# A four-layer graph network on one core: the last two batches' layer-1 projections split and moved, part stores issued by GpSimd, one pace for the list steps

## The chip, the cores and the metric

The kernel runs on one core of a Trainium2 chip. The metric is the device time in microseconds (us) of one execution; the median of three runs stands for a kernel. One further execution is taken with the hardware profiler, and all durations below come from that one.

## The reference, cut to what matters

`x` has 16 batches of 1024 nodes with 256 features in float32; `adj` is 1024 x 1024 with about 17 weighted entries in a row. Four layers follow each other.

```python
# layer 0: a score for every pair (u, v), used only where adj is not zero
hidden = relu(pre_u[:, :, None, :] + pre_v[:, None, :, :] + b1)
S = sigmoid(einsum('buvk,ko->buvo', hidden, W2)[..., 0] + b2[0])
a_t = einsum('buv,bud->bvd', S * A_a, h_t)
z_t = beta1 * h_t + beta2 * (a_t @ Wa + ba) + beta3 * (m_t @ Wm + bm)
# layer 1
msg = einsum('bid,ed->bie', einsum('ij,bjd->bid', A, z), W) + b
z = z + relu(msg)
# layers 2 and 3: softmax over all j of leaky_relu(f1[i] + f1[j]) + adj, then
vals = einsum('bij,bjo->bio', coefs, feats); out = vals + bias2 + data
```

## The kernel before, in words

The 16 batches are worked in four groups of four (`GB = 4`, L20). For each group the scores of layer 0 are computed only for the entries that `adj` has, by a side stream of "list steps" on VectorE, ScalarE and GpSimd (`score_steps`, L717), and scattered into a dense array in DRAM. Beside it TensorE does the matrix work. The `Side` class (L882) mixes the two streams as the program is written: the main stream yields an estimate of its own microseconds, and so many list steps are put in as a pace says.

For a group the main stream does this:

- `with_edges` (L1120) sums the scored edges of layer 0. The node columns are taken in four quarters of 256 (`QN`); in each quarter eight accumulators, that is all eight PSUM banks, take eight blocks of source nodes. Each block is loaded by SyncE (`load_gd`, L904), turned by ScalarE or VectorE (`gc`, L1131 and L1133), and multiplied. After a quarter VectorE adds the eight banks to `z` (L1156).
- `layer_one` (L1206) is layer 1 for two batches: `projected` (L1161) multiplies `z` by the weight of layer 1 into node-major tiles `y`, and `neighbours` (L1189) multiplies `y` by `adj`, whose blocks come from DRAM through SyncE into a pool of three buffers (L1195). `onto` (L1182) applies the relu on ScalarE and adds to `z` on VectorE (L1187).
- `front` (L1004) and `sums` (L1085) are the two attention layers. `sums` has VectorE make weighted tiles `m` (L1099), three ahead (`AHEAD`, L34), which TensorE multiplies. After half of the nodes the ends of `second` or `third` follow.

In the last group (g = 3) there are no scores left to compute, so the side stream is another one. `far_ahead` (L1405) first projects batches 2 and 3 of the group (`projected` with a `keep` that also stores `y` to DRAM, L1408), then does their `neighbours` for the last 256 columns, and then layers 1 to 3 of batches 0 and 1 (`pair_layers`, L1340). Beside these, `by_lists` (L1211) forms the neighbour sums of the first 768 nodes (`FAR = 6` tiles of 128) of batches 2 and 3 by lists: GpSimd gathers rows of the stored `y` by index (L708), VectorE multiplies each by its weight and adds (L1246, L1248). It has 144 steps: 24 for six tiles of extra rows (nodes with more than 16 neighbours), whose sums go to a DRAM array `part_d` by SyncE (L1252), 96 for the six tiles themselves, and 24 that gather from `part_d` and add (L1244). A step's gather is issued four steps ahead (`LEAD`), into a pool of six buffers. The pace is written at L1416: 0.68 steps for each estimated microsecond of the main stream while that stands below 82, then 0.61. When the lists are done, `from_lists` (L1255) turns the sums back through TensorE (L1265), and layers 2 and 3 of batches 2 and 3 end the program.

The `paced` helper (L123) makes an instruction wait for the matrix product that was written some products earlier, six unless another number is given, so that a side stream doesn't run ahead of TensorE. Each engine runs its instructions in order; a DMA waits on the engine that issues it, and what is queued behind it on that engine waits too. A `product` (L130) is in float32 and stands in the trace as two records.

The projection loop as it is, whose place changes:

```python
for jt in range(0, NT, 2):
    for i in range(2):
        ps = bank()
        ... four products of 128x256 into ps ...
        nc.scalar.activation(y[i][:, jt : jt + 2, :], ..., AF.Copy)
        if keep:
            keep(i, slice(jt, jt + 2), y[i][:, jt : jt + 2, :])
```

Of the kernel before, what the change touches and what calls it, by code (L numbers as in the profile page):

```python
# [11 lines left out]
F32 = mybir.dt.float32  # L12
# [5 lines left out]
P = 128  # L18
# [52 lines left out]
def gnn_stack_kernel(  # L71
# [616 lines left out]
    with tc.If(listed > 0) as arm:  # L688
        with ExitStack() as stack:
# [427 lines left out]
            def exponential(jt):  # L1117
                paced(nc.scalar.activation(ea[:, jt, :], ea[:, jt, :], AF.Exp), 16)

            def with_edges(g, hw, z):  # L1120

                doing[0] = "edges"
                for v in range(N // QN):
                    cols = slice(v * QN, (v + 1) * QN)
                    acc = [[bank() for _ in range(DH)] for _ in range(GB)]
                    for ut in range(NT):
                        gd = first_gd.pop(0) if first_gd else load_gd(g, v, ut, back=BACK)
                        gc = gc_pool.tile([P, GB, QN], F32, tag="gc", name="gc")
                        by_batch = gd.rearrange("p n i -> p i n")
                        if ut % 2:  # L1130
                            paced(nc.vector.tensor_copy(gc, by_batch), 16)  # L1131
                        else:
                            paced(nc.scalar.activation(gc, by_batch, AF.Copy), 16)  # L1133
                        for i in range(GB):
                            for eh in range(DH):
                                product(
                                    acc[i][eh][:, :QN], hw[i][:, ut, eh * P : (eh + 1) * P], gc[:, i, :],
                                    start=ut == 0, stop=ut == NT - 1,
                                )
                        if z_loads and ut % 2 == 0:  # L1140
                            load, i = z_loads.pop(0)
                            paced(load(i), 12)
                        if (to_load or to_exp) and ut % 2 and v:
                            if v > 1 and to_exp:
                                exponential(to_exp.pop(0))
                            if to_load:
                                jt = to_load.pop(0)
                                paced(nc.sync.dma_start(ea[:, jt, :], adjT_d[jt]), 16)
                                to_exp.append(jt)
                        yield 3.4 if g or v else 1  # L1150
                    if v == N // QN - 1:
                        while to_exp:
                            exponential(to_exp.pop(0))
                    for i in range(GB):
                        for eh in range(DH):
                            nc.vector.scalar_tensor_tensor(  # L1156
                                z[i][:, eh, cols], acc[i][eh][:, :QN], zbias[:, eh : eh + 1], z[i][:, eh, cols],
                                ALU.add, ALU.add,
                            )

            def projected(z, keep=None):  # L1161

                doing[0] = "one"
                y = [node_major("y") for _ in range(2)]
                for jt in range(0, NT, 2):
                    for i in range(2):
                        ps = bank()
                        for k in range(2):
                            for dh in range(DH):
                                product(  # L1170
                                    ps[:, k * D : (k + 1) * D], z[i][:, dh, (jt + k) * P : (jt + k + 1) * P],
                                    l1wT[:, dh, :], start=dh == 0, stop=dh == DH - 1,
                                )
                        nc.scalar.activation(
                            y[i][:, jt : jt + 2, :], ps.rearrange("p (t d) -> p t d", t=2), AF.Copy
                        )
                        if keep:
                            keep(i, slice(jt, jt + 2), y[i][:, jt : jt + 2, :])
                        yield 1.7
                return y  # L1180

            def onto(z, cols, sums):  # L1182
# [6 lines left out]
            def neighbours(y, z, cols):  # L1189
                doing[0] = "one"  # L1190
                n = cols.stop - cols.start
                acc = [[bank() for _ in range(DH)] for _ in range(2)]
                for jt in range(NT):
                    a = three.tile([P, HN], F32, tag="a", name="adjT_in")[:, :n]
                    nc.sync.dma_start(a, adjT_d[jt][:, cols])  # L1195
                    for i in range(2):
                        for eh in range(DH):
                            product(
                                acc[i][eh][:, :n], y[i][:, jt, eh * P : (eh + 1) * P], a,
                                start=jt == 0, stop=jt == NT - 1,  # L1200
                            )
# [9 lines left out]
            def by_lists(msg):  # L1211

                spares = [gd_pool.tile([P, QN, GB], F32, tag="gd", name="msg") for _ in range(4)]
                halves = [
                    t.rearrange("p n i -> p (n i)")[:, k * 2 * D : (k + 1) * 2 * D] for t in spares for k in range(2)
                ]
                msg.extend(halves[:FAR])
                part = halves[FAR:]
                nc.gpsimd.memset(part[0], 0.0)
                nc.sync.dma_start(part_d[XT * P :, :], part[0])  # L1220

                nc.vector.tensor_scalar(to_u, to_u, float(XT * P), None, ALU.min)
                todo = [(NT + i, k) for i in range(XT) for k in range(QUAD)]
                todo += [(t, k) for t in range(FAR) for k in range(FIRST)]
                todo += [(t, FIRST + q) for t in range(FAR) for q in range(NG)]
                got = {}

                def fetch_row(t, k):
                    z = got[t, k] = slot_pool.tile([P, GB * D], F32, tag="z", name="z")[:, : 2 * D]
                    if t < NT and k >= FIRST:  # L1230
                        at = (k - FIRST) * NT + t
                        gather(z, part_d, to_u[:, at : at + 1])
                    else:
                        gather(z, y_d, lists(t)[1][:, k : k + 1])

                for step in todo[:LEAD]:
                    fetch_row(*step)
                for n, (t, k) in enumerate(todo):
                    if n + LEAD < len(todo):
                        fetch_row(*todo[n + LEAD])  # L1240
                    z = got.pop((t, k))
                    to = msg[t] if t < NT else part[t % len(part)]
                    if t < NT and k >= FIRST:
                        paced(nc.vector.tensor_tensor(to, to, z, ALU.add))  # L1244
                    elif k == 0:
                        paced(nc.vector.tensor_scalar(to, z, lists(t)[3][:, k : k + 1], None, ALU.mult))  # L1246
                    else:
                        paced(nc.vector.scalar_tensor_tensor(  # L1248
                            to, z, lists(t)[3][:, k : k + 1], to, ALU.mult, ALU.add
                        ))  # L1250
                    if t >= NT and k == QUAD - 1:
                        nc.sync.dma_start(part_d[(t - NT) * P : (t - NT + 1) * P, :], to)  # L1252
                    yield

            def from_lists(z, msg):  # L1255
# [146 lines left out]
                if g in finished:  # L1402
                    first_gd.extend(load_gd(g, 0, ut) for ut in range(4))

            def far_ahead(z, main):  # L1405

                both = y_d.rearrange("(t p) (i d) -> p t i d", p=P, i=2)
                y = yield from projected(z, lambda i, ts, y: nc.sync.dma_start(both[:, ts, i, :], y))  # L1408
                gone, far = 0.0, Side(by_lists(msg))
                rest = neighbours(y, z, slice(FAR * P, N))  # L1410

                def slots():
                    nonlocal gone
                    for us in itertools.chain(rest, main):
                        gone += us
                        yield us * (0.68 if gone < 82 else 0.61)  # L1416

                far.along(slots(), dict.fromkeys(PACE, 1))
                for _ in far.steps:
# [147 lines left out]
```

## Time and profile before

| | us |
|---|---|
| median of 3 runs | 3126.28 |
| lowest and highest run | 3121.62, 3131.03 |
| the profiled execution, its time | 3123.77 |
| the profiled execution, its span | 3122.0 |
| TensorE busy in the span | 3071.5 (98%) |
| VectorE busy | 2422.3 (78%) |
| GpSimd busy | 1894.7 (61%) |
| ScalarE busy | 1821.7 (58%) |

A record "PE" is a matrix product, "PEld" the loading of its weights, which runs beside it. "SPq" and "POOLq" are DMAs that SyncE and GpSimd issue. In brackets behind an instruction stands how long its engine had been idle and what ended that. In a table of stretches, "PEclk" is the clock that was granted to TensorE and "DMA share" the mean busy share of the 16 DMA engines. The last group's stretches, in us from the start of the span: edge sums of all four batches 2594 to 2706, projections of batches 2 and 3 to 2720, their last 256 columns to 2735, projections of batches 0 and 1 to 2755, their neighbours to 2811, their layers 2 and 3 to 2962, and layers 2 and 3 of batches 2 and 3 to the end.

### The profile page before, as it was taken

To read this page: it belongs to the slowest core of one execution; us is meant where nothing else is said; L and a number is where in the kernel's file an instruction comes from. 1 tells how busy PE (TensorE), PEld (TensorE's weight loads), DVE (VectorE), ACT (ScalarE), POOL (GpSimd) and SP (SyncE) were. 2 spreads that over 40 slices of the span, in tenths; PEclk is the share of its full clock that TensorE was granted. 3 is DMA by queue.
4 is the path that set the end of the run, shared out by engine and by line. 5 is a ranking of instruction groups with operands and counts; after the bars stand their busy time and mean duration, and the time that the engine had idled before them with its cause. 6 is when DMAs were issued, how large, how long until landed. Compare 5 with 4: busy or idle time off the path is not lost. (4 is left out here: it accounts for less than half of the span.)

```text
span 3122.0 us, 39040 instructions
## 1 busy us (share of the span) xinstructions
PE 3071.5 (98%) x11954; PEld 2181.0 (70%) x11954; DVE 2422.3 (78%) x3247; ACT 1821.7 (58%) x6456; POOL 1894.7 (61%) x1483
## 2 busy tenths in 40 slices
PE   8999999999999999999999999999999999999999
PEld 5544545545547756888875688887568888858888
DVE  7887777778776878999887899988789983257844
ACT  3345555566655766777667677766667762214242
POOL 1156778777665777667677776676777751076600
PEclk9999999999999999999999999999999999999999
DMA  9998888888889777558977655897765554475500
GB/s 322 330 339 302 278 296 266 272 248 254 263 268 347 233 224 209 155 163 279 304 234 214 201 160 166 271 301 236 215 196 157 165 205 158 137 254 158 162 1 28
DMA packets 288420, 699.96 MB, mean 224 GB/s; under 512 B 46141, under 2 KB 141178, under 8 KB 281034
## 3 DMA queue, kind: packets, MB, share of 16 engines
q0 software_dynamic: 128224, 387.80, 42.0%
q1 hardware_dynamic: 132538, 258.46, 23.5%
q10 hardware_dynamic: 27440, 51.13, 4.4%
q8 instruction: 96, 1.57, 0.2%
q14 instruction: 122, 1.00, 0.1%
HBM read 565.83 MB, written 131.41 MB: 223 GB/s over the span
## 5 line engine op out<-in xcount | busy, mean ns | idle before, releaser
L831 ACT ACTIVATE z<-z 128x256 f32<-128x256 f32 x2432 | 979.7, 406 | 585.6 <-DVE z L827 523.0
L825 DVE TENSOR_TENSOR z<-z,u 128x1024 f32<-128x1024 f32 x608 | 738.3, 1219 | 299.1 <-PE bank L131 174.4
L131 PE MATMUL bank<-feats,m 128*128 128x257 f32 x4096 | 908.7, 380 | 1.1 <-ACT feats L1016 0.7
L708 POOL DMA_INDIRECT z<-v_d,slot_v x512 | 665.4, 1300 | 367.1 <-ACT z L831 196.8
L131 PEld LDWEIGHTS bank<-feats,m 128*128 128x128 f32 x4096 | 769.5, 190 | 111.1 <-ACT feats L1016 1.5
L713 POOL DMA_INDIRECT dense_d<-gt,slot_at x512 | 682.5, 1333 | 196.4 <-issue 139.3
L827 DVE SCALAR_TENSOR_TENSOR z<-z,w2r 128x1024 f32<-128x1024 f32 x608 | 737.3, 1219 | 9.3
L131 PE MATMUL bank<-gc,hw 128*128 128x256 f32 x2048 | 451.1, 382 | 14.9 <-ACT gc L1133 10.2
L831 ACT ACTIVATION_READ_ACCUMULATOR z<-z 128x1 f32 x2432 | 461.6, 190 | 0.0
L131 PE MATMUL bank<-adj_sb,h 128*128 128x512 f32 x1024 | 443.0, 592 | 4.4 <-ACT st L333 2.1
L131 PEld LDWEIGHTS bank<-gc,hw 128*128 128x128 f32 x2048 | 388.8, 191 | 76.8 <-ACT gc L1133 13.3
L1099 DVE SCALAR_TENSOR_TENSOR m<-rho,tau,adj_sb 128x512 f32<-128x512 f32 x512 | 375.7, 742 | 66.0 <-PE bank L131 61.7
L131 PE MATMUL bank<-adjT_in,y 128*128 128x512 f32 (+1 forms) x960 | 402.0, 579 | 5.3 <-DMA adjT_in<-adjT_d 3.6
L131 PEld LDWEIGHTS bank<-adj_sb,h 128*128 128x128 f32 x1024 | 194.1, 190 | 244.8 <-issue 239.0
L131 PEld LDWEIGHTS bank<-adjT_in,y 128*128 128x128 f32 x960 | 181.5, 190 | 219.4 <-issue 206.4
L131 PE MATMUL bank<-w,hT 128*128 128x512 f32 (+1 forms) x1024 | 334.0, 486 | 0.0
L131 PEld LDWEIGHTS bank<-w,hT 128*128 128x128 f32 x1024 | 194.5, 190 | 140.9 <-issue 121.9
L1133 ACT ACTIVATE gc<-gd 128x1024 f32<-128x1024 f32 x64 | 133.2, 2082 | 169.9 <-PE bank L131 104.2
L131 PE MATMUL bank<-g_wT,z 128*128 128x257 f32 x1024 | 230.1, 380 | 0.0
L131 PEld LDWEIGHTS bank<-g_wT,z 128*128 128x128 f32 x1024 | 192.2, 190 | 30.0 <-issue 2.9
L708 POOL DMA_INDIRECT z<-v_d,x_node x96 | 125.0, 1303 | 116.8 <-ACT z L831 61.0
L1131 DVE COPY gc<-gd 128x1024 f32<-128x1024 f32 x64 | 71.8, 1122 | 105.8 <-PE bank L131 79.3
(169 smaller groups left out, 2439.1 us busy)
## 6 DMA issues: line engine op xcount, KB each, us to landing
gd<-dense_d SPq DMA_DIRECT2D x128, 512.0 KB
dense_d<-zero ACTq DMA_DIRECT2D x64, 512.0 KB
adjT_in<-adjT_d SPq DMA_DIRECT2D x112, 256.0 KB
h<-in_x_dram SPq DMA_DIRECT2D x19, 1024.0 KB
u_d<-st SPq DMA_DIRECT2D x64, 256.0 KB
v_d<-st SPq DMA_DIRECT2D x64, 256.0 KB
hw_d<-st SPq DMA_DIRECT2D x64, 256.0 KB
u<-u_d POOLq DMA_DIRECT2D x32, 512.0 KB
```

Source lines behind the costliest of these rows:

```text
L131: recent.append(nc.tensor.matmul(*args, **kw))
L708: return nc.gpsimd.indirect_dma_start(out=dst, out_offset=None, in_=src[:], in_offset=bass.IndirectOffsetOnAxis(ap=at, axis=0), **how,)
L713: return nc.gpsimd.indirect_dma_start(out=dst[:], out_offset=bass.IndirectOffsetOnAxis(ap=at, axis=0), in_=src, in_offset=None,)
L825: paced(nc.vector.tensor_tensor(z, z, u, ALU.add))
L827: nc.vector.scalar_tensor_tensor(zk, zk, 0.0, w2r[:, None, :].to_broadcast([P, GB, D]), ALU.max, ALU.mult)
L831: nc.scalar.activation(zk[:, c, :], zk[:, c, :], AF.Copy, accum_out=s[:, k, c : c + 1])
L1099: nc.vector.scalar_tensor_tensor(m, r[:, cols], ta[:, kt : kt + 1], ea[:, kt, cols], ALU.max, ALU.mult)
L1131: paced(nc.vector.tensor_copy(gc, by_batch), 16)
L1133: paced(nc.scalar.activation(gc, by_batch, AF.Copy), 16)
```

## The change

It does four things, the first three in the last group alone.

1. The projection becomes a class with a method `pair(q)` that does two node tiles for both batches. `with_edges` takes a function `between`. In the last group `pair(0)` follows the second quarter of the edge sums and `pair(1)` the third; `pair(2)` and `pair(3)` stay where all four were. Their stores of `y` to DRAM go with them. A `y` tile now holds both batches for half of the node tiles rather than one batch for all; this holds in every group.
2. The sums of the extra rows are stored by GpSimd, three list steps after they are done, instead of by SyncE at once. Their two buffers lie in a tile of the `gc` pool instead of in the fourth tile of the `gd` pool.
3. The gathers from `part_d` follow each tile's own 16 steps, instead of standing at the end for all six tiles.
4. The pace of the list steps is 0.64 for each estimated microsecond throughout.

```diff
-            def with_edges(g, hw, z):
+            def with_edges(g, hw, z, between=None):
...
+                    if between and 0 < v < N // QN - 1:
+                        yield from between(v - 1)
...
-            def projected(z, keep=None):
-
-                doing[0] = "one"
-                y = [node_major("y") for _ in range(2)]
-                for jt in range(0, NT, 2):
+            class Projection:
...
+                def __call__(self, i, jt):
+                    return self.halves[jt // HT][:, i, jt % HT, :]
+
+                def pair(self, q):
+
+                    if q % 2 == 0:
+                        t = ttile("y")[:, : 2 * HT * D]
+                        self.halves.append(t.rearrange("p (i t d) -> p i t d", i=2, t=HT))
                     for i in range(2):
                         ps = bank()
                         for k in range(2):
+                            jt = 2 * q + k
                             for dh in range(DH):
                                 product(
-                                    ps[:, k * D : (k + 1) * D], z[i][:, dh, (jt + k) * P : (jt + k + 1) * P],
+                                    ps[:, k * D : (k + 1) * D], self.z[i][:, dh, jt * P : (jt + 1) * P],
                                     l1wT[:, dh, :], start=dh == 0, stop=dh == DH - 1,
                                 )
...
+                        nc.scalar.activation(y, ps.rearrange("p (t d) -> p t d", t=2), AF.Copy)
+                        if self.keep:
+                            self.keep(i, slice(2 * q, 2 * q + 2), y)
                         yield 1.7
...
-                part = halves[FAR:]
+                free = gc_pool.tile([P, GB, QN], F32, tag="gc", name="part").rearrange("p i n -> p (i n)")
+                part = [free[:, : 2 * D], free[:, 2 * D :]]
...
-                todo += [(t, k) for t in range(FAR) for k in range(FIRST)]
-                todo += [(t, FIRST + q) for t in range(FAR) for q in range(NG)]
-                got = {}
+                todo += [(t, k) for t in range(FAR) for k in range(FIRST + NG)]
+                got, done = {}, []
...
                     if t >= NT and k == QUAD - 1:
-                        nc.sync.dma_start(part_d[(t - NT) * P : (t - NT + 1) * P, :], to)
+                        done.append((n + 3, t - NT, to))
+                    if done and n == done[0][0]:
+                        _, at, of = done.pop(0)
+                        nc.gpsimd.dma_start(part_d[at * P : (at + 1) * P, :], of)
                     yield
...
-            def far_ahead(z, main):
-
-                both = y_d.rearrange("(t p) (i d) -> p t i d", p=P, i=2)
-                y = yield from projected(z, lambda i, ts, y: nc.sync.dma_start(both[:, ts, i, :], y))
+            def far_ahead(z, y, main):
+
+                doing[0] = "one"
+                for q in range(NT // 2 - 2, NT // 2):
+                    yield from y.pair(q)
                 gone, far = 0.0, Side(by_lists(msg))
...
-                        yield us * (0.68 if gone < 82 else 0.61)
+                        yield us * 0.64
...
-                side.along(with_edges(g, hw, z))
+                y = None
+                if g == NGR - 1:
+                    both = y_d.rearrange("(t p) (i d) -> p t i d", p=P, i=2)
+                    y = Projection(z[2:], lambda i, ts, y: nc.sync.dma_start(both[:, ts, i, :], y))
+                side.along(with_edges(g, hw, z, y and y.pair))
...
-                    for _ in far_ahead(z[2:], pair_layers(g * GB, z[:2], layer_one(z[:2]))):
+                    for _ in far_ahead(z[2:], y, pair_layers(g * GB, z[:2], layer_one(z[:2]))):
```

More of the change, by code (lines that the diff above doesn't have):

```diff
@@ L1159, in with_edges, with __init__ @@
                             )
-            def projected(z, keep=None):
-                doing[0] = "one"
-                y = [node_major("y") for _ in range(2)]
-                for jt in range(0, NT, 2):
+                    if between and 0 < v < N // QN - 1:
+                        yield from between(v - 1)
+            class Projection:
+                def __init__(self, z, keep=None):
+                    self.z, self.keep, self.halves = z, keep, []
+                def __call__(self, i, jt):
[4 more added lines that the diff above has]
+                        self.halves.append(t.rearrange("p (i t d) -> p i t d", i=2, t=HT))
                     for i in range(2):
@@ L1168, in projected @@
                         for k in range(2):
+                            jt = 2 * q + k
                             for dh in range(DH):
                                 product(
-                                    ps[:, k * D : (k + 1) * D], z[i][:, dh, (jt + k) * P : (jt + k + 1) * P],
+                                    ps[:, k * D : (k + 1) * D], self.z[i][:, dh, jt * P : (jt + 1) * P],
                                     l1wT[:, dh, :], start=dh == 0, stop=dh == DH - 1,
                                 )
[L1174 to L1178, printed above, removed]
-                        yield 1.7
+                        at = 2 * q % HT
+                        y = self.halves[-1][:, i, at : at + 2, :]
+                        nc.scalar.activation(y, ps.rearrange("p (t d) -> p t d", t=2), AF.Copy)
+                        if self.keep:
+                            self.keep(i, slice(2 * q, 2 * q + 2), y)
+                        yield 1.7
+            def projected(z):
+                doing[0] = "one"
+                y = Projection(z)
+                for q in range(NT // 2):
+                    yield from y.pair(q)
                 return y
@@ L1198, in neighbours @@
                             product(
-                                acc[i][eh][:, :n], y[i][:, jt, eh * P : (eh + 1) * P], a,
+                                acc[i][eh][:, :n], y(i, jt)[:, eh * P : (eh + 1) * P], a,
                                 start=jt == 0, stop=jt == NT - 1,
@@ L1403, in soon @@
                     first_gd.extend(load_gd(g, 0, ut) for ut in range(4))
-            def far_ahead(z, main):
-                both = y_d.rearrange("(t p) (i d) -> p t i d", p=P, i=2)
-                y = yield from projected(z, lambda i, ts, y: nc.sync.dma_start(both[:, ts, i, :], y))
+            def far_ahead(z, y, main):
+                doing[0] = "one"
+                for q in range(NT // 2 - 2, NT // 2):
+                    yield from y.pair(q)
                 gone, far = 0.0, Side(by_lists(msg))
```

## The prediction

> **What bounds the kernel now.** I began with the page's head, then took the table of stretches for the last group, then the order in time of TensorE, and last the queues' order and waits where TensorE stood still.
>
> ```profile
> span 3122.0 us, 39040 instructions
> PE 3071.5 (98%) x11954; PEld 2181.0 (70%) x11954; DVE 2422.3 (78%) x3247; ACT 1821.7 (58%) x6456; POOL 1894.7 (61%) x1483
> ```
>
> TensorE is the bound: 50.5 us of the whole span are without it. The change removes no product, so what it can win is idle time of TensorE. The chain of waits shows only its last pieces and says nothing here. The stretches of 10 us around the projections:
>
> ```profile
> 2730.00:2740.00 10.00, 9.51 (x45) 8.07 (x44) 3.73 (x7) 1.77 (x4) 7.62 (x8) 1.00 0.86 276
> 2740.00:2750.00 10.00, 6.39 (x24) 4.59 (x23) 5.28 (x11) 2.02 (x4) 5.40 (x6) 0.89 0.75 254
> 2750.00:2760.00 10.00, 10.00 (x33) 6.46 (x32) 5.92 (x10) 2.44 (x5) 7.56 (x9) 0.94 0.73 218
> 2760.00:2770.00 10.00, 8.52 (x20) 3.42 (x18) 3.43 (x5) 0.00 (x0) 7.87 (x8) 1.00 0.91 320
> ```
>
> Columns: stretch, us, busy TensorE, weight loads, VectorE, ScalarE, GpSimd, granted clock, DMA share, GB/s. The DMA engines are at 73 to 91%, and after the hole at 2740 the clock is below 1. TensorE's order in time there:
>
> ```profile
> 2706.61 13.98 PE L131 MATMUL bank<-l1wT,z 128*128 128x256 f32 x64
> 2720.43 10.52 PE L131 MATMUL bank<-adjT_in,y 128*128 128x256 f32 x48
> 2731.44 3.69 PE L131 MATMUL bank<-adjT_in,y 128*128 128x256 f32 x16 [0.49 <-DMA adjT_in<-adjT_d]
> 2734.97 8.58 PE L131 MATMUL bank<-l1wT,z 128*128 128x256 f32 x39
> 2744.30 0.38 PE L131 MATMUL bank<-l1wT,z 128*128 128x256 f32 x1 [0.75 <-issue]
> 2746.39 0.38 PE L131 MATMUL bank<-l1wT,z 128*128 128x256 f32 x1 [1.72 <-issue]
> 2747.78 7.01 PE L131 MATMUL bank<-l1wT,z 128*128 128x256 f32 x23 [1.01 <-issue]
> 2754.63 13.90 PE L131 MATMUL bank<-adjT_in,y 128*128 128x512 f32 x32
> 2770.04 41.54 PE L131 MATMUL bank<-adjT_in,y 128*128 128x512 f32 x96 [1.52 <-issue]
> ```
>
> A record of 256 columns costs 13.82 / 64 = 0.216 us (first line to second), one of 512 columns 0.432. From 2720.43 to 2811.42, where the fronts begin, 128 x 0.216 + 128 x 0.432 = 82.9 us of work take 91.0: **8.1 us are lost**. Hole C (rest of the columns): 14.5 for 13.8, 0.7. Hole A (projections): 19.7 for 13.8, 5.9. Hole B (neighbours): 56.8 for 55.3, 1.5. Elsewhere in the group little is idle, so 8.1 us, 0.26%, is all that these parts can give back in this execution.
>
> What stood at SyncE (order in time, then its waits from 2700 to 2830):
>
> ```profile
> 2762.90 0.32 SPq L1252 DMA_DIRECT2D part_d<-msg  x1
> ...
> 2763.33 40.05 SPq L1195 DMA_DIRECT2D adjT_in<-adjT_d  x12
> ```
>
> ```profile
> SPq L1252 <- DVE msg L1248: 12.3, 3, 5.7
> SPq L1195 <- remote: 4.8, 1, 4.8
> ```
>
> The part stores hold SyncE for 12.3 us (the 4.8 below belong to hole A), and `adjT_in` loads are behind them. The block used at 2770.04 was asked for at 2763.33, behind the store at 2762.90; its buffer was free at about 2754.63 + 2 x 3.46 = 2761.5. So B is 1.8 us of held queue, shown. A isn't shown so: in it no product waits for a DMA, and ScalarE (2743.5 to 2748.6), VectorE (2743.9 to 2748.5) and SyncE stand too, while the DMA share is high. I take it for an effect of too many transfers at once: a gather issued at 2738.81 was used at 2748.54, 9.7 us later.
>
> **What the Trainium skill says.** "TensorE: Matmul & The Clock Gate", Part 1 (the HAM clock gate): after some 3.4 us of idleness the array runs at half rate, until some 3.4 us of work. The trace agrees: 0.89 and 0.94 in the two stretches above are 1.7 us of lost clock, so A is 4.2 us of standing and 1.7 of slow clock; a shorter hole would cost less than in proportion. "DMA: Bandwidth & Descriptors", Queues, rings and completion order: each DMA engine goes round between the queue rows packet by packet, and a ring is taken in order. A store moved from SyncE to GpSimd thus stands behind the gathers; no row of before shows that. Same page, Anatomy of one DMA: about 2.0 us and bytes / 436e3 us, so 2.6 us for 256 KB with nothing else under way; the first gather here took 3.6 (2724.13 to 2727.70).
>
> **The change part by part.**
>
> *Pairs 0 and 1 between quarters.* A pair is 8 products or 16 records, 3.46 us; two are 6.9 us of TensorE moved, none removed: 0. Is anything won at the seams of quarters? Records there follow at 0.216 (48 in 10.52 us across 2645.75 and 2673.81), so nothing. Is anything lost? The order of the built program puts each pair behind a quarter's last products. It takes two of the eight banks, which VectorE frees first (L1156, 3.5 us for eight); its two ScalarE copies of 0.60 us end about 4.2 us after the seam, and the next quarter wants those banks back at 3.46 + 6 x 0.43 = 6.0. ScalarE's `gc` copies before and after are due at -3.4 and +6.9 us. Each pair brings two stores to SyncE, between `gd` loads; they wait for ScalarE until +2.4 and +4.2, while the loads behind them may start at +3.5 and +6.9 only, so none is held. DMA share is 0.45 there; 0.5 MB more at a seam fits. I take 0; if a load came late it would be 1 to 2 us at each of two seams.
>
> *After the edges* two pairs (6.9 us) remain ahead of the list steps' start rather than four. The lists wait for the last `y` store in both kernels, so their start stands as before to the neighbours: no gain, no loss.
>
> *Part stores by GpSimd.* SyncE loses six waits: B goes, -1.5 us. GpSimd takes 6 x 1.01 us (its row for `u<-u_d`), hidden in its idle time (13.0 busy of 20 us). The store doesn't hold GpSimd: it comes three steps late, behind a gather that needed a later step. But VectorE reuses a half eight steps after, and waits for the store: it is issued about one gather (1.25 us) after step 4i+4, and reused at step 4i+8, 3 steps of 1.56 = 4.7 us. So up to S = 3.4 us it is free; beyond, four reuses (steps 8, 12, 16, 20) cost S - 3.4 each. S lies between 2.6 (skill) and 9.7 (slowest gather); I take 5.5, a gather from 2732.55 to 2738.02: 4 x 2.1 = 8.4 us of lag in the lists, at most 25. Queued behind on VectorE are the adds of L1187, for which nobody waits yet. Cost on the path: 0, as long as the lag is gone when `sums` needs VectorE (third rival).
>
> *Gathers from `part_d` inside the tiles.* 24 as before, of the same size. The first is issued ten steps (some 15 us) after the last store: 0.
>
> *Pace.* The main stream's estimates sum to 227.5 us; 144 steps took 82 + (144 - 55.8) / 0.61 = 226.6 of them, and take 144 / 0.64 = 225. The last add ends at 2960.94, TensorE wants it at 2962.36: 1.6 us more room, no gain. At first 6% fewer gathers are asked for, 0.04 x 256 KB, some 10 of 250 KB/us less.
>
> *`y` halves in other groups.* Same matmuls, copies and waits in the built order: 0.
>
> *Hole A.* Bounds: 0 and -5.9. For its end: fewer steps at first, stores that slow VectorE and with it the gathers, `adjT_in` loads let go some 8 us sooner. Against: the bytes are the same. I take it as gone. C stays: the same loads into the same three buffers.
>
> Sum: -1.5 - 5.9 = **-7.4** on the profiled execution's 3123.8 (span 3122.0 and 1.8 around it): 3116.4. The median of before stands 2.5 above that execution, so on it 3126.3 - 7.4 = **3118.9**.
>
> **The rivals.** *A returns.* Bytes and engines are the same and nothing shows what stopped the engines: only B goes, 3126.3 - 1.5 = 3124.8. *The seams cost:* 2 x 2 us and A stays: 3128.8. *The lists fall behind* (slower): VectorE runs in order, and if it still lags when `sums` begins, TensorE waits for `m`. The lists start with 7.3 us of lag (2720.43 to 2727.70, as now), reuses add 4 (S - 3.4); 37 steps lie between step 24 and `sums` (95 estimated us x 0.64 = 61 steps), each can catch up 1.56 - 1.25 = 0.31 us: 11.5. Three tiles ahead cover 5.2 (1.73 each). It decides from S = 5.75 us, close to what I take. At S = 9.7 it costs 7.3 + 25 - 11.5 - 5.2 = 15.6, and A would hardly go: 3140. For it speaks the slow gather, against it that a late VectorE itself thins out the gathers, so that stores run freer.
>
> **How the numbers follow.** A and B gone, 3118.9: 0.50. A returns, 3124.8: 0.30. Seams, 3128.8: 0.06. Lists behind, 3140: 0.14. Half the spread of three runs is 4.7 us, so the low end is 3118.9 - 4.7, about 3114, and the high end 3124.8 + 4.7, about 3130, leaving out the lists. A measurement of this kernel can tell about 0.3% (9.4 us) from no change, so faster begins at 3116.9: half of the first case, 0.25; slower begins at 3135.7: most of the last, 0.13; same 0.62.
>
> **What would show it.** Right: no SyncE part stores and no hole above 1 us in TensorE between the rest columns and the fronts, clock 1.00 there; seams at 0.216 a record. B wrong: an `adjT_in` wait of 1.5 us remains. A returns: several engines stop together under a DMA share near 0.9. Lists behind: L1264 waits for `part_d` stores, then TensorE for `m`. Wrong altogether: TensorE idle at a seam, or idle time won outside the last group.

## The result, and the profile after

In twenty runs of each the median is 3117.11 us after (3110.94 to 3122.41) and 3127.64 us before (3115.39 to 3135.46). The ratio on record is 0.9973, with a 95% interval of 0.9964 to 0.9982: 8.4 us faster, between 5.6 and 11.3. (It isn't the quotient of the two medians, which lie 10.5 us apart; that quotient, 0.9966, is inside the interval.) The forecast was 3118.9. The profiled execution after took 3116.69 us, against 3123.77 before.

The page's head after, and the order in time of TensorE in the last group:

```profile
span 3115.0 us, 39031 instructions
PE 3070.9 (99%) x11954; PEld 2181.2 (70%) x11954; DVE 2424.0 (78%) x3247; ACT 1823.5 (59%) x6456; POOL 1899.5 (61%) x1489
```

```profile
2652.69 3.62 PE L131 MATMUL bank<-l1wT,z 128*128 128x256 f32 x16
2656.14 27.79 PE L131 MATMUL bank<-gc,hw 128*128 128x256 f32 x128
...
2714.85 7.07 PE L131 MATMUL bank<-l1wT,z 128*128 128x256 f32 x32
2721.76 10.52 PE L131 MATMUL bank<-adjT_in,y 128*128 128x256 f32 x48
2732.68 3.82 PE L131 MATMUL bank<-adjT_in,y 128*128 128x256 f32 x16 [0.40 <-DMA adjT_in<-adjT_d]
2736.34 13.98 PE L131 MATMUL bank<-l1wT,z 128*128 128x256 f32 x64
2750.15 55.10 PE L131 MATMUL bank<-adjT_in,y 128*128 128x512 f32 x128
2805.09 8.85 PE L131 MATMUL bank<-g_wT,z 128*128 128x257 f32 x40
```

TensorE is busy for 3070.9 us as before (3071.5) and the span is 7.0 shorter, so idle time went. (The two traces aren't equally complete, which bears on the projections; see below.) From 2721.76, where the last 256 columns start, to the first front at 2805.09 are 83.3 us for 82.9 us of work: 0.4 lost, where before it was 8.1. The projections of batches 0 and 1 take 13.8 (19.7 before), the neighbours 54.9 (56.8 before); only the small hole of the columns is left. That is -7.7. The edges began 1.1 later (2595.65 against 2594.56), took 0.2 more, and what follows the fronts took 0.7 less: -7.0, the whole difference of the spans. The two pairs at the seams take 3.45 us each (2652.69 to 2656.14), and no idle time stands beside them.

The stretches there after, with the columns of the table of before:

```profile
2730.00:2740.00 10.00, 9.60 (x44) 7.97 (x43) 3.50 (x5) 2.37 (x6) 7.86 (x8) 1.00 0.84 254
2740.00:2750.00 10.00, 10.00 (x48) 8.80 (x47) 6.35 (x12) 3.57 (x6) 7.95 (x9) 1.00 0.81 259
2750.00:2760.00 10.00, 10.00 (x25) 4.50 (x24) 4.65 (x7) 0.60 (x1) 8.09 (x9) 1.00 0.77 244
2760.00:2770.00 10.00, 10.00 (x25) 4.47 (x24) 4.68 (x7) 0.00 (x0) 7.66 (x9) 1.00 0.84 295
```

The clock is 1.00 throughout. But the DMA engines are as full as before, 77 to 84% against 73 to 91%: nothing says that the holes went because fewer bytes were under way.

SyncE's waits from 2700 to 2830 after (what was waited for, us in total, times, longest):

```profile
SPq L1213 <- PE bank L131: 63.6, 21, 16.8
SPq L1239 <- POOL part L1238: 10.2, 1, 10.2
```

The 12.3 us behind part sums are gone; what SyncE waits for at L1213 is a buffer that TensorE has yet to free, as it should be. The 10.2 us are the store of zeros into `part_d`, which waits until GpSimd has filled its half in the `gc` pool; it goes at 2712.24, ahead of the first `y` store behind the edges at 2717.40, and nothing stands behind it. Where the new wait went, in VectorE's waits, then in the list of DMA issues (KB each, median us from issue to landing), then in VectorE's order in time:

```profile
DVE part L1264 <- DMA part_d<-part: 9.6, 4, 4.2
```

```profile
part_d<-part POOLq DMA_DIRECT2D x6, 256.0 KB, 5.2
```

```profile
2756.56 0.51 DVE L1264 TENSOR_SCALAR part<-z,x_a 128x512 f32<-128x512 f32 x1 [4.23 <-DMA part_d<-part]
```

A store takes 5.2 us and VectorE waits for four of them, 9.6 us in all. TensorE doesn't feel it here.

### The profile page after: what moved, and what is told of

It is laid out like the page before. It is cut to its first block, busy times and chain, and to the rows that moved or that the text cites. A ratio compares the mean times of both kernels' runs of the same rounds, so it can differ in the third digit from the quotient of the medians.

```text
span 3115.0 us, 39031 instructions
## 1 busy us (share of the span) xinstructions
PE 3070.9 (99%) x11954; PEld 2181.2 (70%) x11954; DVE 2424.0 (78%) x3247; ACT 1823.5 (59%) x6456; POOL 1899.5 (61%) x1489
## 3 DMA queue, kind: packets, MB, share of 16 engines
q8 instruction: 96, 1.57, 0.2%
```

## The experiments

The twelve experiments come in three sets (e1 to e4; e5 to e7 and e9; e8 and e10 to e12), each beside runs of the kernel before on the same chip, whose medians are 3126.7, 3130.0 and 3133.3. So only the ratios are compared. "Lost" is TensorE's time from the start of the last 256 columns to the first front, less the 82.9 us of work, in the one profiled execution of each. The last columns say where it was lost: C the columns, A the projections, B the neighbours.

| kernel | ratio to before (95%) | lost | C | A | B |
|---|---|---|---|---|---|
| the change | 0.9973 [0.9964, 0.9982] | 0.4 | 0.8 | 0 | -0.4 |
| e1 after, stores by SyncE at once | 0.9995 [0.9984, 1.0007] | 5.3 | 0.5 | 0 | 4.7 |
| e2 after, stores by SyncE late | 0.9997 [0.9986, 1.0007] | 1.6 | 0.6 | 0 | 0.9 |
| e3 after, old pace | 0.9988 [0.9975, 1.0000] | 0.2, and 4.1 in the front | 0.5 | 0 | -0.4 |
| e4 after, pairs not moved | 0.9978 [0.9968, 0.9988] | 0.4 | 0.8 | 0 | -0.4 |
| e5 before, stores by GpSimd | 0.9992 [0.9981, 1.0003] | 7.1 | 0.8 | 1.4 | 5.0 |
| e6 after, four halves | 0.9979 [0.9967, 0.9991] | 2.0 | 0.5 | 0 | 1.5 |
| e7 after, part gathers last | 0.9988 [0.9975, 1.0001] | 2.9 | 0.8 | 1.4 | 0.8 |
| e8 before, one pace | 0.9991 [0.9978, 1.0004] | 6.7 | 0.7 | 6.3 | -0.4 |
| e9 before once more | | 7.2 | 0.7 | 0 | 6.5 |
| e10 before, five blocks | 0.9991 [0.9976, 1.0005] | 7.7 | 0 | 6.7 | 1.0 |
| e11 after, five blocks | 0.9991 [0.9975, 1.0007] | 1.6 | 0 | 1.9 | -0.4 |
| e12 before, half the bytes | 1.0003 [0.9991, 1.0014] | 6.5 | 5.6 | 0 | 0.9 |

C and A are counted against 13.8 us each and B against 55.3; a B of -0.4 is one without any hole (54.9). The intervals are about as wide as the effects, so a single pair of ratios often doesn't part two kernels, and the traces have to help. Each trace is one execution.

**Were the holes there at all, in another execution?** e9 is the kernel before, unchanged, with one more profile.

> The kernel before, a second look. If hole A belongs to the program, 4 to 6 us are lost in the projections of batches 0 and 1 again. If it comes and goes from run to run (the runs of the kernel before spread over 20 us, those of the changed kernel over 11), this look shows another loss, between 1 and 8 us in the stretch from the last 256 columns to the first front, perhaps in another place.

TensorE's order in time, then SyncE's:

```profile
2735.15 13.98 PE L131 MATMUL bank<-l1wT,z 128*128 128x256 f32 x64
2748.96 10.46 PE L131 MATMUL bank<-adjT_in,y 128*128 128x512 f32 x24
2763.14 47.76 PE L131 MATMUL bank<-adjT_in,y 128*128 128x512 f32 x104 [3.71 <-DMA adjT_in<-adjT_d]
```

```profile
2745.51 11.98 SPq L1252 DMA_DIRECT2D part_d<-msg  x3
2757.60 0.37 SPq L1195 DMA_DIRECT2D adjT_in<-adjT_d  x1
```

The sum is nearly the same, 7.2 for 8.1, but it lies elsewhere: hole A, the largest term of the prediction, isn't there, and hole B is 6.5 us instead of 1.5. Three part stores stand ahead of one load of `adjT_in` in SyncE's order; the product that needs the load starts 5.5 us after it is issued. How the loss splits into A and B differs from one execution to the next; its sum was about the same in these two.

**Are the profiles of one kind?** They aren't, and it bears on hole A. A trace also records the signals (semaphore updates) by which an engine tells the others that an instruction is done. In the traces of after and e1 to e4 the signals of TensorE are complete: 4219 in after, for 4219 products that send one. In before and e5 to e12 about one in eight is missing: 3707 of 4216 in before. The pages show it in their lists of DMA issues: the line of `u<-u_d` ends with a time to landing, 8.7 us, in after, and has none in before.

In the incomplete traces signals also come late: 52 to 83 of TensorE's came more than 0.3 us after the last product that could have sent them, 11 to 30 of these between 2590 and 2830 us. The complete ones have two each, none of them there. Every hole A of the table, large or small, is in an incomplete trace, and of the kernels built on before there is no complete one. So the table can't tell whether the change removed A or whether A comes and goes with the kind of the trace. The incomplete executions aren't long ones (3123.77 us for before, whose median is 3127.64), so whether the timed executions have such holes stays open. After and e1 to e4 can be compared with each other, and there loss and ratio go together: 0.4 us (after, e4) at 0.9973 and 0.9978, 4.3 (e3) at 0.9988, 5.3 (e1) at 0.9995; only e2 is out of line.

**Who moves the stores?** e1 gives them back to SyncE at once, e2 to SyncE three steps late; all else is as in the change. e5 is the other way round: only the move to GpSimd, in the kernel before.

```diff
 # e1, against after
-                        done.append((n + 3, t - NT, to))
-                    if done and n == done[0][0]:
-                        _, at, of = done.pop(0)
-                        nc.gpsimd.dma_start(part_d[at * P : (at + 1) * P, :], of)
+                        nc.sync.dma_start(part_d[(t - NT) * P : (t - NT + 1) * P, :], to)
 # e2, against after
-                        nc.gpsimd.dma_start(part_d[at * P : (at + 1) * P, :], of)
+                        nc.sync.dma_start(part_d[at * P : (at + 1) * P, :], of)
 # e5, against before
-                        nc.sync.dma_start(part_d[(t - NT) * P : (t - NT + 1) * P, :], to)
+                        done.append((n + 3, t - NT, to))
+                    if done and n == done[0][0]:
+                        _, at, of = done.pop(0)
+                        nc.gpsimd.dma_start(part_d[at * P : (at + 1) * P, :], of)
```

> The changed kernel with its part stores issued by SyncE as soon as each sum is done, as before the change; pairs, order of gathers and pace stay changed. Theory 'held queue' (hole B, and A with it, come from part stores that hold SyncE with adjT_in loads behind them): B comes back with 1 to 2 us of TensorE idle in the neighbours of batches 0 and 1, A perhaps too; ratio to the kernel before 0.9980 (only B back) to 1.0. Theory 'crowding' (A comes from the number of gathers asked for, so the pace cures it): B back, A not; 0.9978. Theory 'placing' (moving two pairs cures both): no hole, 0.9973.

> The changed kernel with its part stores three steps late as they are, but issued by SyncE. Theory 'held queue': the sum is long done when the store's turn comes, unless SyncE gets there early; SyncE reaches the store as soon as the load before it is issued, so it still waits, now for a step three later if it waits at all. Prediction: the same six stores stand before the same adjT_in loads, but wait only for their own sum, so that holding is as long as in e1; hole B 1 to 2 us, ratio 0.998. If the ring of GpSimd is what matters (stores in order with the gathers slow VectorE down and so thin out the gathers), A comes back here and in e1: 1.0.

> The kernel before with one part of the change alone: part stores by GpSimd, three steps late. Pairs, order of gathers and the pace 0.68 then 0.61 are those of before. 'Held queue': holes A and B go, but the store waits put VectorE behind at the old pace, so a wait of the first front for the adds to z (as in e3, 2.0 us and slow clock after it) is likely; ratio 0.9980 to 0.9990. 'Crowding' as the cause of A: A stays, ratio 0.9995.

e1, SyncE's wait for VectorE from 2700 to 2830, its order in time, and the product that waited:

```profile
SPq L1270 <- DVE part L1266: 22.7, 5, 5.9
```

```profile
2754.09 6.57 SPq L1270 DMA_DIRECT2D part_d<-part  x2
2760.77 0.88 SPq L1213 DMA_DIRECT2D adjT_in<-adjT_d  x2
```

```profile
2766.45 46.60 PE L131 MATMUL bank<-adjT_in,y 128*128 128x512 f32 x104 [3.13 <-DMA adjT_in<-adjT_d]
```

That is e9's picture again, in a kernel that has every other part of the change, and in a complete trace. The load's buffer was free at about 2756.3, when the first block's eight records were done (2752.85 + 3.46). The second of the two stores went at 2760.34, when VectorE's sum had just ended (2760.31), and the load at 2760.77, some 4.5 us late. Both e1 and e2 lose the gain (0.9995 and 0.9997; their intervals begin at 0.9984 and 0.9986, that of the change ends at 0.9982), so stores off SyncE are needed. e2's profile shows only 1.6 us lost, less than its ratio asks for; that execution, 3116.79 us, is one of the two fastest of its fourteen (median 3124.82). In it SyncE still waits 20.0 us behind sums of VectorE.

Whether they are enough, e5 leaves open. Its ratio, 0.9992, can't be told from 1, and its interval begins at 0.9981, just where that of the change ends. SyncE holds no part store any more, and yet the block used at 2774.69 came late:

```profile
2762.00 10.46 PE L131 MATMUL bank<-adjT_in,y 128*128 128x512 f32 x24
2774.69 39.66 PE L131 MATMUL bank<-adjT_in,y 128*128 128x512 f32 x88 [2.23 <-DMA adjT_in<-adjT_d]
```

```profile
SPq L1195 <- remote: 3.9, 1, 3.9
```

The load was issued at 2769.34, though the buffer's last product ended at about 2765.5 (2762.00 + 3.5); the 3.9 us between are a wait whose end the view can't put to any engine of the core ("remote"). The signals show more: TensorE ran without a gap from 2762.00 to 2772.46, but its signals are on record in ones to threes at 2765.63, 2767.80, 2768.58, 2769.32 and 2770.77, and the load went at once after the one at 2769.32. So it waited for a late signal of TensorE, and not for a store. Such signals are in incomplete traces alone, so the 5.0 us of B here say little about the edit.

**Does the lag of VectorE matter?** e3 takes the old pace into the change, e6 removes the reuse wait by two more halves, e7 puts the gathers from `part_d` back to the end, e8 has the new pace alone in the kernel before.

```diff
 # e3, against after; e8 is the reverse, against before
-                        yield us * 0.64
+                        yield us * (0.68 if gone < 82 else 0.61)
 # e6, against after
-                free = gc_pool.tile([P, GB, QN], F32, tag="gc", name="part").rearrange("p i n -> p (i n)")
-                part = [free[:, : 2 * D], free[:, 2 * D :]]
+                free = [
+                    gc_pool.tile([P, GB, QN], F32, tag="gc", name="part").rearrange("p i n -> p (i n)")
+                    for _ in range(2)
+                ]
+                part = [f[:, k * 2 * D : (k + 1) * 2 * D] for f in free for k in range(2)]
 # e7, against after
-                todo += [(t, k) for t in range(FAR) for k in range(FIRST + NG)]
+                todo += [(t, k) for t in range(FAR) for k in range(FIRST)]
+                todo += [(t, FIRST + q) for t in range(FAR) for q in range(NG)]
```

> The changed kernel with the old pace, 0.68 then 0.61. 'Crowding': more gathers early, A comes back in part or whole, TensorE loses 2 to 6 us between the rest columns and the fronts, ratio 0.9985 to 0.999. 'Held queue' and 'placing': as the changed kernel, 0.9973.

> The changed kernel with four part buffers in place of two, so that VectorE no longer waits for a store before it reuses one. If these waits only cost lag that is worked off before the fronts: ratio as the changed kernel, 0.9973, no VectorE wait for part_d stores, lists on pace some 10 us sooner. If the waits are what thins out the gathers and keeps hole A away ('crowding'): A returns, 0.999.

> The changed kernel with all 24 gathers from part_d at the end of the lists, as before the change. They are as many and as large: ratio as the changed kernel, 0.9973, and no hole. If their place matters, the end of the lists shows it: TensorE waits for the last msg before the turn back of the sums.

> The kernel before with one edit: the list steps' pace is 0.64 throughout. If transfers crowded together are the cause of the lost time, 6% fewer gathers at first should thin the holes: ratio 0.998 to 0.999, 3 to 5 us lost between the start of the last 256 columns and the first front. If the cause is SyncE held behind the part stores, nothing goes: ratio 0.9995 to 1.0005, 6 to 8 us lost, and VectorE still in SyncE's waits for some 12 us. I take the second as likelier, since the pace alone leaves the stores where they were.

e3, TensorE from the end of the neighbours, then VectorE:

```profile
2751.47 55.10 PE L131 MATMUL bank<-adjT_in,y 128*128 128x512 f32 x128
2806.41 3.64 PE L131 MATMUL bank<-g_wT,z 128*128 128x257 f32 x16
2812.04 7.33 PE L131 MATMUL bank<-g_wT,z 128*128 128x257 f32 x24 [2.00 <-DVE z L1205]
2819.21 1.04 PE L1062 MATMUL bank<-ident,feats 128*128 128x128 f32 x8
```

```profile
2810.64 0.75 DVE L1266 SCALAR_TENSOR_TENSOR msg<-z,slot_a,msg 128x512 f32<-128x512 f32 x1 [0.80 <-DMA z<-y_d,slot_v]
2811.30 1.93 DVE L1205 TENSOR_TENSOR z<-z,r 128x512 f32<-128x512 f32 x3
```

The stretch is whole (0.2 lost), but the first front takes 12.8 us from 2806.41 to 2819.21 where the change takes 8.7 (2805.09 to 2813.78). The front needs `z` after the adds of L1205, and these are queued on VectorE behind list steps that still wait for their gathers, 1.5 us each. In the change the same adds begin at 2803.43, 1.7 us before the front starts; here 4.9 after it:

```profile
2803.43 0.69 DVE L1205 TENSOR_TENSOR z<-z,r 128x512 f32<-128x512 f32 x1 [0.78 <-ACT r L1204]
```

With more steps asked for at first the lists are thus some 6.5 us later against the front. Of the 4.1 us, 2.0 are standing; the rest is TensorE at half its clock, which the trace grants from 2813.65 for 3.4 us. e6 has no wait for a store at all, and its ratio (0.9979) can't be told from that of the change: at the pace of 0.64 the 9.6 us of waits cost nothing that shows. e7 (0.9988) can't be told from the change by its interval; its trace lost 1.4 us in A and 0.8 in B. e8 had all of hole A (2.45 us of standing, and a clock of 0.66 in the stretch from 2750) and no B, at 0.9991. So with the pace alone (e8) and with the stores alone (e5) holes were seen, but in incomplete traces. Each is worth some 0.001 of the ratio, which no interval here parts from nothing.

**Is anything won by moving the pairs?** e4 puts all four pairs back behind the edges.

```diff
-                    if between and 0 < v < N // QN - 1:
+                    if False:
...
-                for q in range(NT // 2 - 2, NT // 2):
+                for q in range(NT // 2):
```

> The changed kernel with all four pairs after the edge sums, as before the change; stores, order and pace stay changed. 'Placing': holes A and B come back, ratio 1.0. 'Held queue' and 'crowding': no holes, 0.9973; the seams cost nothing, so nothing moves but the place of 6.9 us.

```profile
2723.93 10.52 PE L131 MATMUL bank<-adjT_in,y 128*128 128x256 f32 x48
2734.97 3.69 PE L131 MATMUL bank<-adjT_in,y 128*128 128x256 f32 x16 [0.51 <-DMA adjT_in<-adjT_d]
2738.50 13.98 PE L131 MATMUL bank<-l1wT,z 128*128 128x256 f32 x64
2752.31 55.10 PE L131 MATMUL bank<-adjT_in,y 128*128 128x512 f32 x128
```

TensorE's order in time in e4 shows the same loss as the change (0.4 us), and its ratio is nearly the same, 0.9978. The part of the change that needs most code is worth nothing that can be measured.

**Late loads, or too many bytes?** e10 gives the `adjT_in` blocks of the last group five buffers instead of three in the kernel before, e11 does it in the change. e12 stores, gathers and sums batch 2 alone; its sums stand for batch 3 too, whose own listed sums are left out.

```diff
 # e10 against before, e11 the same against after
-                    a = three.tile([P, HN], F32, tag="a", name="adjT_in")[:, :n]
+                    if more_a and jt % 5 > 2:
+                        a = more_a[jt % 5 - 3][:, :n]
+                    else:
+                        a = three.tile([P, HN], F32, tag="a", name="adjT_in")[:, :n]
...
+                wide_a = gc_pool.tile([P, GB, QN], F32, tag="gc", name="more_a").rearrange("p i n -> p (i n)")
+                more_a.extend([wide_a[:, :HN], wide_a[:, HN:]])
 # e12, against before
-    y_d = dram.tile([N, 2 * D], F32, name="y_d")
-    part_d = dram.tile([XT * P + P, 2 * D], F32, name="part_d")
+    y_d = dram.tile([N, D], F32, name="y_d")
+    part_d = dram.tile([XT * P + P, D], F32, name="part_d")
...
-                    z = got[t, k] = slot_pool.tile([P, GB * D], F32, tag="z", name="z")[:, : 2 * D]
+                    z = got[t, k] = slot_pool.tile([P, GB * D], F32, tag="z", name="z")[:, :D]
```

> The kernel before with five buffers for the adjT_in blocks instead of three in the last group, so that a load is asked for two blocks earlier. If the holes are loads that land late, whatever makes them late (a held SyncE or crowded DMA engines), a lead of 3.5 to 7 us more hides them: no wait of TensorE for adjT_in from the second block on, 1 to 2 us lost, ratio about 0.9975. If the loss is engines standing together under crowded transfers, with no load waited for, more lead doesn't help or adds to the crowding: 6 us or more lost and ratio about 1.000.

> The changed kernel with five buffers for the adjT_in blocks instead of three in the last group. If what remains in the changed kernel are loads that land late now and then (0.4 us in its first profile), this takes it away: ratio to the kernel before 0.996 to 0.997, loss under 0.5 us. If more loads under way at once slow the gathers, the lists lag and the first front waits for an add of L1205: ratio 0.998 or more.

> The kernel before with the lists at half their bytes: only batch 2's y is stored, gathered and summed, and its sums stand for batch 3 too, so batch 3's listed sums are left out. The part stores stay on SyncE and the pace stays. If the lost time comes from the number of bytes under way, it goes: under 2 us lost in the stretch, ratio about 0.997. If it comes from SyncE standing behind the part stores, VectorE still has to finish each sum first (its adds are half as long): 4 us or more lost, ratio 0.999 or more. The second half of the lists' adds falls away on VectorE as well, so a gain beyond 8 us would be VectorE's and not the transfers'.

In e10 hole C is gone and hole A is there in full. The order in time of all engines inside A (PEld is the weight load):

```profile
2748.76 0.19 PEld L131 LDWEIGHTS bank<-l1wT,z 128*128 128x128 f32 x1 [0.55 <-issue]
...
2749.45 0.38 PE L131 MATMUL bank<-l1wT,z 128*128 128x256 f32 x1 [0.86 <-issue]
...
2750.17 0.19 PEld L131 LDWEIGHTS bank<-l1wT,z 128*128 128x128 f32 x1 [1.22 <-issue]
...
2751.58 1.50 PE L131 MATMUL bank<-l1wT,z 128*128 128x256 f32 x2 [1.75 <-issue]
2752.28 0.29 PEld L131 LDWEIGHTS bank<-l1wT,z 128*128 128x128 f32 x1 [1.93 <-issue]
2752.30 0.49 DVE L1251 TENSOR_SCALAR msg<-z,x_a 128x512 f32<-128x512 f32 x1 [1.83 <-remote]
...
2753.74 2.29 PE L131 MATMUL bank<-l1wT,z 128*128 128x256 f32 x5 [0.66 <-issue]
...
2753.76 0.60 ACT L1174 ACTIVATE y<-bank 128x512 f32<-128x512 f32 x1 [8.70 <-PE bank L131]
```

No load is waited for here, so more lead doesn't help, and A and B are different things. C is loads that came late, since five buffers remove it. e11 is no better than the change: 0.9991, its interval wide, 1.6 us lost in a small hole A. Its profiled execution was late before the last group already (the edges began at 2609.10), where the edit does nothing.

In e12 the DMA engines are at 46 to 61% from 2730 to 2770 (73 to 91% before). Hole A isn't there, and yet nothing is gained: 1.0003. TensorE and SyncE in time:

```profile
2722.42 10.52 PE L131 MATMUL bank<-adjT_in,y 128*128 128x256 f32 x48
2736.61 5.38 PE L131 MATMUL bank<-adjT_in,y 128*128 128x256 f32 x16 [3.66 <-issue]
2741.82 13.98 PE L131 MATMUL bank<-l1wT,z 128*128 128x256 f32 x64
...
2770.55 41.44 PE L131 MATMUL bank<-adjT_in,y 128*128 128x512 f32 x96 [1.02 <-DMA adjT_in<-adjT_d]
```

```profile
2732.11 0.32 SPq L1252 DMA_DIRECT2D part_d<-msg  x1
2732.53 1.50 SPq L1195 DMA_DIRECT2D adjT_in<-adjT_d  x3
```

The three loads were let go only after a part store at 2732.11, just behind the end of VectorE's sum at 2732.08, and the product that follows starts 4.1 us later. (The view names nothing for its wait, "issue"; that it waited for the load is read from the order in time.) With half the bytes the held queue of SyncE costs 5.6 us in this one place.

## Why the prediction was right, step by step

- *B goes, -1.5.* The mechanism is right and its size too small. The load behind the store, and the store behind VectorE, are seen in e1 and e9, and in e12 by the order in time. The 1.5 was what one execution showed. Where part stores stand on SyncE, B was 1.5, 6.5 (e9), 4.7 (e1), 1.0 (e10), 0.9 (e2, e12) and none in e8, and C was 5.6 in e12. e1 differs from the change in nothing but these stores, both traces are complete, and it loses 4.9 us more; its ratio is 0.0022 higher, some 7 us. So the held queue can carry most of the measured gain.
- *A goes, -5.9.* **Not shown, and the sum came out near by luck.** The trace of after has no A, but that of before, from which the 5.9 come, is incomplete and that of after is not. Among the incomplete traces, of the kernels built on before, A was seen in full in before, e8 and e10, small in e5, and not in e9 and e12; of those built on the change it was small in e7 and e11 and missing in e6. That is a hint and no more. "I take it for an effect of too many transfers at once" isn't borne out either: A was missing with half the bytes (e12), but in e9 too, with all of them, and in after the DMA share is unchanged. If A isn't the change's doing, 3 to 5 us too little for B (4.7 and 6.5 for 1.5) and 5.9 too much for A have largely cancelled.
- *C stays.* Right: 0.8 for 0.7. Five buffers remove it (e10, e11).
- *Clock.* The prediction takes a stand of 3.4 us as what halves the clock, and says that a shorter hole costs less than in proportion. Here less was enough: half the clock followed a stand of 2.00 us in e3 and one of 2.45 in e8, and e3's 2.0 us of standing cost 4.1. After 1.61 us in e6 the clock stayed at 1.00.
- *Seams, 0.* Right: 3.45 us a pair, no idle time, and e4 shows no gain either. The lists' start stands as predicted, 7.4 us from the start of the columns to the first add (2721.76 to 2729.20) against 7.3.
- *GpSimd's store, 1.01 us.* It takes 0.6 and is hidden.
- *S, 5.5.* Measured 5.2 (median). The estimate of 2.6 from the formula of the Trainium skill ("DMA: Bandwidth & Descriptors", Anatomy of one DMA) is half of that. The page names no load there, so "with nothing else under way" is the prediction's own reading of it. The waits were 9.6 us for 8.4.
- *Cost on the path, 0.* Right as far as e6 can tell, and near the point named. 9.6 / 4 + 3.4 makes an S of 5.8, just past the 5.75 from which the lists were to fall behind, and they did not.
- *Pace, "1.6 us more room, no gain".* **This step failed in e3's trace.** The working looked at the end of the lists, and for the lag at `sums`. It also said that nobody waits for the adds of L1187 queued on VectorE. That holds for those of the last 256 columns; those of batches 0 and 1's neighbours (L1205 after) are waited for by the first front. With the old pace the lag comes out there, 4.1 us. The ratio is 0.9988 for 0.9973, but the intervals overlap (0.9975 to 1.0000 and 0.9964 to 0.9982), so that the timed runs lose by it is likely and not shown. The rival "the lists fall behind" is real, at another place and at a fifth of its price (4.1 of 21 us).

The predicted -7.4 lies inside the measured 5.6 to 11.3, and the profiled executions are 7.1 apart. As a number it held; of its two terms, B was too small and A isn't shown to be the change's doing. Of the four parts, the stores need to leave SyncE (e1, e2). Whether that is enough is open (e5); the pace is likely to be needed with it (e3); the order of the gathers is undecided (e7), and the moved pairs do nothing that can be measured (e4).

## What to carry to other kernels

A store on an in-order queue that waits for a late engine holds every load behind it; move it to another queue, and then ask who reuses the store's buffer and what is queued behind that wait. When the main engine's idle time is a handful of small holes, take a second profile of the same kernel before pricing each: the sum was steady here (8.1 and 7.2), the parts weren't (A 5.9 and 0, B 1.5 and 6.5). Before you set two profiles side by side, see that the records of both are complete, for instance that their pages give times to landing for the same DMAs. If a side stream lags, look for the first thing on its engine that the main stream needs, not for the stream's own end.

## What was not expected of the hardware

Inside hole A most restarts of several engines lie on one beat. In e10 a weight load, a product, a VectorE add and a ScalarE copy start at 2748.76, 2749.45, 2750.17, 2751.58, 2752.28, 2752.30, 2753.74 and 2753.76: steps of 0.69 to 0.73 us or twice that, and two engines within 0.02 us of each other. The same beat is in the profile of before (weight loads and products at 2745.69, 2746.39, 2747.09, 2747.78 and 2748.49) and in e8.

The traces' records of signals say what was held. In before not one signal of TensorE is on record from 2742.88 to 2748.51, and then twelve come within 0.5 us; in e8 there is one between 2748.55 and 2753.53, and then again twelve within 0.5 us. In e5, where TensorE's products ran on from 2762.00 to 2772.46, its signals came at steps of 0.70 to 0.78 us or two or three times that. So the signals were held up and the engines that wait for them stood; what TensorE itself waited for in hole A isn't on record. All this is in traces that miss one signal in eight, and in none of the five complete ones. Whether the recording held the signals up, or both have another cause, was not tried. (The instructions themselves come by DMA: the page after counts 96 packets and 1.57 MB on one such queue, 122 packets and 1.00 MB on another. Whether late packets of these have a part in it is open too.)
